# Moving the weighting of gathered pixels to ScalarE, parts of softplus to VectorE, and the order of the last image

## The chip, the cores and the metric

The kernel runs on one core of a Trainium2 chip. The core has five engines that run beside each other[...]: TensorE (PE, matrix products into PSUM), VectorE (DVE), ScalarE (ACT), GpSimd (POOL), and SyncE (SP, which here only issues transfers). Transfers are also issued from the queues of ACT and POOL. Each engine takes its instructions in the order in which the program lists them; one that waits holds up all behind it on the same engine. The metric is the time of one execution on the device in microseconds. The kernel before takes 9075.24 us, the median of nine runs between 9048.84 and 9094.0.

## The reference, cut to what matters

The input is four images of 96 channels and 64 x 64 pixels, so L = 4096 positions. Four layers are added to it in turn.

- Layer 0 normalises, projects to 192 channels, applies a 3 x 3 convolution and then a selective scan along four directions (rows, columns, and both reversed). With softplus written out, a step of it is

```
delta = softplus(dts + bias)          # max(p, 0) + log(1 + exp(-|p|))
h     = exp(delta * A) * h + (delta * u) * B      # 16 states per channel
y     = sum over the states of h * C
```

- Layer 1 is a deformable 3 x 3 convolution: for every pixel and each of nine taps an offset and a mask are computed, four neighbouring pixels are fetched and weighted, and the weighted sum goes through the weights of the tap:

```
samp = (1-wy)*(1-wx)*v00 + (1-wy)*wx*v01 + wy*(1-wx)*v10 + wy*wx*v11      # times the mask
out += einsum('bchw,oc->bohw', samp, weight[:, :, i, j])                   # for each of 9 taps
```

- Layer 2 is a Fourier transform along the positions with a pointwise network in it, then a feed-forward network whose operands are rounded to an 8-bit float. Layer 3 is a linear attention, then a second feed-forward network of the same kind.

## The kernel before, in words

**The scan sets the frame.** Layer 0's recurrence is cut into 1536 units: 4 images x 4 directions x 4 steps of 1024 positions x 24 groups of 8 channels x 16 states (128 partitions). For a unit, ACT fetches `da` (a transfer that repeats delta over the states) and takes its exponential (`decay`, L933), PE spreads delta times u into PSUM (`inflow`, L939), DVE multiplies by B in place (`enter`, L953) and runs the recurrence (`recur`, L961), POOL multiplies by C (`weigh`, L970, and the copy of the last state, L968), and PE sums over the states (`total`, L989). `hh`, the scan's output, has six buffers and `da` six; `db` in PSUM has two.

**Two streams lie beside it.** `ends()` runs `before` of layer 0 for images 0 to 3 (normalisation, convolution, projection, `steps`), and then layers 2 and 3 of image 0, 1, 2, 3 in turn. `middle()` runs, for each image, `behind` (the end of layer 0) and layer 1: `offsets`, `positions` and `sample`. An image can enter layers 2 and 3 only when layer 1 has sampled it.

**A planner writes the order.** The program's order on every engine is written when it is built. A `Clock` holds the planned end of each of PE, DVE, ACT and POOL; a step of a stream carries its planned cost (`cost(...)`), and is put in when the clock has room for it (`has_room`). A unit of the scan moves the clock on by at least `PACE`. The constant and the costs are not waits: they decide only which instructions stand between two units. What the streams have not done when the 1536 units are over stands after the scan, in the same manner (`alone`, `own_banks` is then set). `go()` offers the streams a step, `middle` first.

**`steps` (L752 to L815)** makes delta and delta times u for 512 positions of one direction (or of two half directions). PE gives the pre-activation `pd`; ACT takes |p|, exp, log(1 + e) into `lw`, 1 + e into `w1` and then `w1` - 1; POOL takes `w1` - e (the rounding of 1 + e, L780) and `lw` minus it (L781); DVE makes `rl` = max(p, 0) + `lw` (L783); POOL multiplies it by u into `ex` (L786 or L792); ACT and PE split that into three 16-bit parts. There are 192 such chains: 4 images x 8 pieces x 6. Nine of them start before the first unit of the scan.

**`sample` (L1284 to L1354)** handles an image in 96 chains, each of 128 pixels and three taps. POOL issues three indirect transfers (L1301), each of which brings 128 x 384 numbers (four neighbours x 96 channels) into `g`; one DVE multiplication over 128 x 1152 numbers applies the twelve weights per pixel (L1310); PE turns the result and adds the four neighbours (L1327), after the scan DVE adds them itself (L1314, L1315); ACT copies it to `st` (L1335). After six chains the nine taps are multiplied by the weights (L1343).

**The feed-forward networks (L1556 to L1600)** handle 512 positions at a time. POOL rounds the input to 8 bits (L1567) and the hidden values too (L1585).

Of the kernel before, what the change touches and what calls it, by code (L numbers as in the profile page):

```python
# [8 lines left out]
F32 = mybir.dt.float32  # L9
# [5 lines left out]
AF = mybir.ActivationFunctionType  # L15
ALU = mybir.AluOpType
# [184 lines left out]

MARGIN = 0.5

PACE = 4.7


class Clock:
# [138 lines left out]
class Net:  # L346
# [3 lines left out]
    def __init__(self, ctx, tc, ins):  # L350
        self.tc, self.nc, self.ins = tc, tc.nc, ins
        nc = self.nc
        self.const = ctx.enter_context(tc.tile_pool(name="const", bufs=1))
        self.dram = ctx.enter_context(tc.tile_pool(name="scratch", bufs=1, space=DRAM))
        self.psum = ctx.enter_context(tc.tile_pool(name="mm", bufs=3, space=PSUM))
        for name in ("vecs", "ident", "cen96", "grp3", "add4"):
            setattr(self, name, self.load(name, self.const))

        self.to_row = {}
        for n in (C, DI):  # L360
            t = self.to_row[n] = self.const.tile([128, 65], F32, name=f"to_row{n}")
            nc.vector.memset(t, 0.0)
            nc.vector.memset(t[:, 1:2], 1.0 / n)
        self.eps = self.const.tile([128, 1], F32, name="eps")
        nc.vector.memset(self.eps, 1e-5)
        self.one = self.const.tile([128, 1], F32, name="one")
        nc.vector.memset(self.one, 1.0)
        self.minus_one = self.const.tile([128, 1], F32, name="minus_one")
        nc.vector.memset(self.minus_one, -1.0)
        self.exp_and_log()  # L370

        self.sampled = set()
        self.clock, self.known, self.streams, self.stream = Clock(), {}, [], None

        self.own_banks = None
# [164 lines left out]
class Layer0:  # L540
# [211 lines left out]
    def steps(self, b, ks, j, us, dtw, sm, xdbl):  # L752

        net = self.net
        nc = net.nc
        cs = slice(j * CH, (j + 1) * CH)
        tk = f"{b}_{j}_" + "".join(str(k) for k in ks)
        both = len(ks) == 2

        def tile_of(name, bufs):  # L760
            return sm.tile([128, CH], F32, name=f"{name}{tk}", tag=name, bufs=bufs)

        yield wait(new=True, takes="ex lw")


        pd = net.mm(f"pd{tk}")
        for k in ks:
            q = k % 2
            o, m = (pd[64 * q : 64 * q + 64], slice(128, DI)) if both else (pd, slice(0, 128))
            nc.tensor.matmul(o, lhsT=dtw[:, k, m], rhs=xdbl[q, j], start=True, stop=True)  # L770
        ex = tile_of("ex", 3)
        nc.scalar.activation(ex, pd, AF.Abs)
        nc.scalar.activation(ex, ex, AF.Exp, scale=-1.0)
        lw, w1 = tile_of("lw", 1), tile_of("w1", 1)
        nc.scalar.activation(lw, ex, AF.Ln, bias=net.one)
        nc.scalar.activation(w1, ex, AF.Identity, bias=net.one)
        nc.scalar.activation(w1, w1, AF.Identity, bias=net.minus_one)  # L777
        yield cost(pe=2.2 if both else 1.1, act=3.4, holds=1, takes="rl")
        rl = tile_of("rl", 2)
        nc.gpsimd.tensor_sub(w1, w1, ex)  # L780
        nc.gpsimd.tensor_sub(lw, lw, w1)  # L781
        yield cost(pool=2.8, holds=1)
        nc.vector.scalar_tensor_tensor(rl, pd, 0.0, lw, ALU.max, ALU.add)  # L783
        yield cost(dve=0.7, frees="lw")
        if not both and ks[0] % 2:
            nc.gpsimd.tensor_mul(  # L786
                ex.rearrange("p (w h) -> p w h", h=H),
                rl.rearrange("p (w h) -> p w h", h=H),
                us[1][:, j * NR : (j + 1) * NR, :],
            )  # L790
        else:
            nc.gpsimd.tensor_mul(ex, rl, us[2 if both else 0][:, cs])  # L792
        parts = ((0, 64, ks[0], 128), (64, 128, ks[1], 128)) if both else ((0, 128, ks[0], 0),)
        for p0, p1, k, c0 in parts:
            nc.sync.dma_start(self.de_d[b][k][c0 : c0 + p1 - p0, cs], rl[p0:p1])
        yield cost(pool=1.4, takes="du", frees="rl")

        du = sm.tile([128, 3, CH], BF16, name=f"du{tk}", tag="du", bufs=2)
        nc.scalar.copy(du[:, 0, :], ex)
        yield cost(act=0.6, new=True)  # L800
        pr = net.mm(f"pr{tk}")
        nc.tensor.matmul(pr, lhsT=net.ident, rhs=ex, start=True, stop=False)  # L802
        nc.tensor.matmul(pr, lhsT=self.minus, rhs=du[:, 0, :], start=False, stop=True)
        nc.scalar.copy(du[:, 1, :], pr)
        yield cost(pe=1.5, act=0.6, holds=1, frees="ex")
        nc.tensor.matmul(
            pr, lhsT=self.minus, rhs=du[:, 1, :], start=False, stop=True, skip_group_check=True
        )
        nc.scalar.copy(du[:, 2, :], pr)
        yield cost(pe=0.4, act=0.6)  # L810
        for p0, p1, k, c0 in parts:
            dst = self.du_d[b][k][:, c0 : c0 + p1 - p0, cs]
            nc.sync.dma_start(dst.rearrange("s c t -> c s t"), du[p0:p1])
        self.ready.update((b, k, both, j) for k in ks)
        yield wait(frees="du")  # L815
# [300 lines left out]
class Layer1:  # L1116
# [23 lines left out]
    def image(self, b):  # L1140
        tc = self.net.tc
        with tc.tile_pool(name=f"l1i{b}", bufs=1, side="right") as ix:
            idx = ix.tile([128, 288], U32, name=f"idx{b}", tag="idx")
            wt = ix.tile([128, 288, 4], F32, name=f"wt{b}", tag="wt")
            yield from self.before(b, idx, wt)
            yield from self.sample(b, idx, wt)
        self.net.sampled.add(b)

# [135 lines left out]
    def sample(self, b, idx, wt):  # L1284
        net = self.net
        tc, nc = net.tc, net.nc
        with tc.tile_pool(name=f"l1g{b}", bufs=1, side="right") as gp:
# [4 lines left out]
            def taps(t, k0):  # L1292
# [6 lines left out]
                for k in range(3):  # L1299
# [5 lines left out]
                        in_offset=bass.IndirectOffsetOnAxis(ap=idx[:, n : n + 1], axis=0),  # L1305
                    )
                    yield cost(pool=1.5, wait=7.0 * (k == 2))
                g4 = g.rearrange("p k (c d) -> p (k c) d", d=C)
                w4 = wt[:, 9 * t + k0 : 9 * t + k0 + 3, :].rearrange("p k c -> p (k c)")
                nc.vector.tensor_mul(g4, g4, w4.unsqueeze(2).to_broadcast([128, 12, C]))  # L1310
                added = net.own_banks is not None
                if added:

                    nc.vector.tensor_add(g[:, :, : 2 * C], g[:, :, : 2 * C], g[:, :, 2 * C :])  # L1314
                    nc.vector.tensor_add(g[:, :, :C], g[:, :, :C], g[:, :, C : 2 * C])  # L1315
                first = q == 0 and k0 == 0
                yield cost(dve=2.7 if added else 1.8, new=True, takes="st" if first else "")
                if first:
                    sts[j] = gp.tile([C, 9, 256], F32, name=f"st{b}_{j}", tag="st")
                st = sts[j]  # L1320
# [210 lines left out]
class Ffn:  # L1531
# [23 lines left out]
    def run(self, b, t):  # L1555
        net, n = self.net, self.n  # L1556
        tc, nc = net.tc, net.nc
        with tc.tile_pool(name=f"fb{n}_{b}", bufs=1) as big, tc.tile_pool(name=f"fs{n}_{b}", bufs=2) as pool:
# [3 lines left out]
            def chunk(j):  # L1562
# [1 line left out]
                cs = slice(j * CH, (j + 1) * CH)  # L1564
                key = f"f{n}_{b}_{j}"
                xq = pool.tile([C, CH], F8, name=f"xq{key}", tag="xq")
                nc.gpsimd.tensor_copy(xq, tl[:, cs], saturate=False)  # L1567
                yield cost(pool=0.8, new=True, takes="h16")
                h16 = pool.tile([128, 3, CH], F16, name=f"h16{key}", tag="h16")
                for g in range(3):  # L1570
                    ph = net.mm(f"ph{key}_{g}")
# [10 lines left out]
                        nc.scalar.activation(h16[:, g], h16[:, g], AF.Relu, bias=self.bias[:, g : g + 1])  # L1582
                    yield cost(act=2.1, takes="h8")
                h8 = pool.tile([128, 3, CH], F8, name=f"h8{key}", tag="h8")
                nc.gpsimd.tensor_copy(h8, h16, saturate=False)  # L1585
                yield cost(pool=1.5, new=True, takes="o16", frees="h16")
                po = net.mm(f"po{key}")
                for g in range(3):
                    nc.tensor.matmul(po, lhsT=self.w2[:, g, :], rhs=h8[:, g], start=(g == 0), stop=(g == 2))
# [107 lines left out]
def layers23(net, x2, out):  # L1697
# [4 lines left out]
    with ExitStack() as ctx:  # L1702
# [21 lines left out]

        def go():

            return any([stream.step() for stream in reversed(streams)])

        def alone():

# [44 lines left out]
```

## Time and profile before

| | |
|---|---|
| median of nine runs | 9075.24 us |
| the profiled execution: its own time, and its span | 9094.23 us, 9092.4 us |
| busy: PE, DVE, ACT, POOL | 6614.3, 6969.0, 4183.0, 6363.9 us |
| first unit's recurrence starts, last one ends | 369 us, 7900 us |
| image 3: `offsets` starts, first gather, last operation of `sample` | 7955, 8071, 8539 us |
| transfer that loads image 3 for layers 2 and 3 starts | 8634 us |

The page of a profile gives for each group of instructions its line, engine and operation, the tiles it writes and reads, and then the busy time, the mean duration in ns, the idle time of the engine just before and what ended most of it. A table of stretches gives the busy time of each engine within a stretch of the span, then the granted TensorE clock, the share of the transfer engines and GB/s.

The trace shows three stages: up to 370 us layer 0 of the first image without the scan, up to 7900 us the scan with the streams beside it, and then some 1190 us of what is left.

### The profile page before, as it was taken

To read this page: it belongs to the slowest core of one execution; us is meant where nothing else is said; L and a number is where in the kernel's file an instruction comes from. 1 tells how busy PE (TensorE), PEld (TensorE's weight loads), DVE (VectorE), ACT (ScalarE), POOL (GpSimd) and SP (SyncE) were. 2 spreads that over 40 slices of the span, in tenths; PEclk is the share of its full clock that TensorE was granted. 3 is DMA by queue.
4 is the path that set the end of the run, shared out by engine and by line. 5 is a ranking of instruction groups with operands and counts; after the bars stand their busy time and mean duration, and the time that the engine had idled before them with its cause. 6 is when DMAs were issued, how large, how long until landed. Compare 5 with 4: busy or idle time off the path is not lost.

```text
span 9092.4 us, 93197 instructions
## 1 busy us (share of the span) xinstructions
PE 6614.3 (73%) x31960; PEld 2990.0 (33%) x31960; DVE 6969.0 (77%) x4932; ACT 4183.0 (46%) x5798; POOL 6363.9 (70%) x4755
## 2 busy tenths in 40 slices
PE   6664977697766668777667877777777677875687
PEld 2111311132222234211224554223454332463373
DVE  0367878887788889788789898988999999636514
ACT  4564667565554435556543334554333434321223
POOL 0486678766789989788799895765888967537501
PEclk8675977798778779877778888878888887876797
DMA  1466778777778788887778878677888776644210
GB/s 51 127 184 168 191 193 221 200 188 191 196 205 212 203 207 219 196 207 213 200 206 203 226 204 193 169 166 198 209 216 213 190 175 177 152 131 135 76 55 12
DMA packets 775967, 1608.21 MB, mean 177 GB/s; under 512 B 247809, under 2 KB 339357, under 8 KB 773382
## 3 DMA queue, kind: packets, MB, share of 16 engines
q10 hardware_dynamic: 244224, 843.17, 36.9%
q1 hardware_dynamic: 457542, 532.51, 21.8%
q0 software_dynamic: 73728, 226.57, 9.4%
q8 instruction: 255, 4.18, 0.2%
q14 instruction: 218, 1.79, 0.1%
HBM read 1345.62 MB, written 256.29 MB: 176 GB/s over the span
## 4 chain that ended last, share of the span: by engine, by line
PE 32%; DVE 20%; DMA 17%; POOL 12%; issue 10%; ACT 6%; SPq 2%; ACTq 1%; another core or an unknown queue 0%; DVEq 0%; POOLq 0%
DVE hh L961 9%; DVE db L953 6%; POOL hh L970 5%; PE pc L692 4%; PE ps L1327 3%; PE py L989 3%; PE f L1421 3%; PE db L939 3%; DMA du<-du 3%; DMA da<-de 3%; POOL g L1301 2%; PE pd L1343 2%; DVE g L1310 2%; DMA m<-in_dft 1%; PE pd L770 1%
## 5 line engine op out<-in xcount | busy, mean ns | idle before, releaser
L970 POOL TENSOR_TENSOR hh<-hh,bc 128x1024 f32<-128x1024 f32 x1536 | 3654.9, 2382 | 353.3 <-DVE hh L961 239.2
L961 DVE TENSOR_TENSOR_SCAN hh<-da,st,db 128x1024 f32<-128x1024 f32 x1152 | 2700.7, 2344 | 177.9 <-PE py L989 47.0
L953 DVE TENSOR_TENSOR db<-db,bc 128x1024 f32<-128x1024 f32 x1536 | 1864.5, 1214 | 511.7 <-PE db L939 497.8
L933 ACT ACTIVATE da<-da,w_al 128x1024 f32<-128x1024 f32 x1536 | 1739.7, 1147 | 843.4 <-DMA da<-de 383.1
L939 PE MATMUL db<-du,rep 96*128 96x512 bf16 x3072 | 1092.5, 445 | 791.8 <-DVE hh L961 711.9
L1301 POOL DMA_INDIRECT g<-table,idx x1152 | 1326.9, 1152 | 380.9 <-issue 227.0
L989 PE MATMUL py<-hh,w_fold 128*32 128x512 f32 x6144 | 1089.8, 741 | 85.1 <-POOL hh L970 57.7
L1327 PE MATMUL ps<-w_ident,g 128*96 128x128 f32 x3744 | 640.8, 334 | 504.1 <-issue 282.2
L961 DVE TENSOR_TENSOR_SCAN hh<-da,db 128x1024 f32<-128x1024 f32 x384 | 876.9, 2284 | 60.7 <-PE py L989 23.1
L939 PEld LDWEIGHTS <-rep 96*128 96x128 bf16 x3072 | 279.3, 106 | 1755.5 <-issue 1129.9
L1327 PEld LDWEIGHTS ps<-w_ident,g 128*96 128x96 f32 x3744 | 520.4, 155 | 780.2 <-issue 408.3
L1310 DVE TENSOR_TENSOR g<-g,wt 128x1152 f32<-128x1152 f32 x384 | 716.0, 1866 | 67.0 <-DMA g<-table,idx 62.6
L1335 ACT COPY st<-ps 96x384 f32<-96x384 f32 x384 | 181.8, 476 | 1271.4 <-PE ps L1327 1027.1
L968 POOL COPY st<-hh 128x1 f32<-128x1 f32 x1152 | 294.3, 255 | 509.6 <-DVE hh L961 464.9
L780 POOL TENSOR_TENSOR w<-w,ex 128x512 f32<-128x512 f32 x192 | 245.1, 1276 | 505.4 <-ACT w L777 504.7
L692 PE MATMUL pc<-pad,wc 96*128 96x512 f32 x1152 | 540.8, 609 | 48.3 <-DMA wc<-wc_d 44.0
L783 DVE SCALAR_TENSOR_TENSOR rl<-pd,lw 128x512 f32<-128x512 f32 x192 | 131.3, 684 | 425.7 <-POOL lw L781 411.1
L802 PE MATMUL pr<-ex,w_ident 128*128 128x512 f32 x384 | 290.8, 849 | 150.5 <-POOL ex L786 67.4
L1567 POOL CAST xqf<-fl 96x512 fp8e5<-96x512 f32 x64 | 46.9, 741 | 497.5 <-DVE fl L1525 458.8
L989 PEld LDWEIGHTS py<-hh,w_fold 128*32 128x32 f32 x6144 | 160.6, 120 | 606.4 <-issue 384.7
L770 PE MATMUL pd<-xd,w_dtw 103*64 103x512 f32 (+1 forms) x512 | 276.9, 817 | 65.8 <-DMA w_dtw<-in_dtw 33.1
L692 PEld LDWEIGHTS pc<-pad,wc 96*128 96x128 f32 x1152 | 215.8, 193 | 318.6 <-issue 295.9
(249 smaller groups left out, 9231.4 us busy)
## 6 DMA issues: line engine op xcount, KB each, us to landing
da<-de ACTq DMA_DIRECT2D x1536, 512.0 KB
du<-du SPq DMA_DIRECT2D x512, 192.0 KB
bc<-bcd SPq DMA_DIRECT2D x128, 512.0 KB
du<-du SPq DMA_DIRECT2D x128, 384.0 KB
y<-yb SPq DMA_DIRECT2D x384, 128.0 KB
de<-rl SPq DMA_DIRECT2D x128, 256.0 KB
m<-in_dft SPq DMA_DIRECT2D x128, 256.0 KB
ad<-y ACTq DMA_DIRECT2D x192, 128.0 KB
```

What stands on the lines that cost most here:

```text
L692: nc.tensor.matmul(pp, lhsT=wc[:, q, g * 128 : (g + 1) * 128], rhs=pad[:, r0 + dy : r0 + dy + NR, dx : dx + W], start=(q == 0), stop=(q == 8),
L770: nc.tensor.matmul(o, lhsT=dtw[:, k, m], rhs=xdbl[q, j], start=True, stop=True)
L933: self.net.nc.scalar.activation(u.da, u.da, AF.Exp, scale=self.al[:, a : a + 1])
L939: self.net.nc.tensor.matmul(db[:, h, :], lhsT=self.rep[:96, u.s % 4, :], rhs=u.du[u.s // 4][:, h * CH : (h + 1) * CH], start=True, stop=True,)
L953: self.net.nc.vector.tensor_mul(u.db, u.db, u.bc[:, 0, :])
L961: nc.vector.tensor_tensor_scan(u.along(u.hh), u.along(u.da), u.along(u.db), first, ALU.mult, ALU.add)
L968: self.net.nc.gpsimd.tensor_copy(u.state[:, u.n : u.n + 1], u.hh[:, last : last + 1])
L970: self.net.nc.gpsimd.tensor_mul(u.hh, u.hh, u.bc[:, 1, :])
L989: nc.tensor.matmul(py[p0 : p0 + 32], lhsT=self.fold[:, u.i, :], rhs=hc[:, h * CH : (h + 1) * CH], start=u.sums["add"] is None and u.i == 0 ...
L1301: nc.gpsimd.indirect_dma_start(out=g[:, k, :], out_offset=None, in_=self.tables[b % 2], in_offset=bass.IndirectOffsetOnAxis(ap=idx[:, n : ...
L1310: nc.vector.tensor_mul(g4, g4, w4.unsqueeze(2).to_broadcast([128, 12, C]))
L1327: nc.tensor.matmul(pt[:, k, :], lhsT=g[:, k, c * C : (c + 1) * C], rhs=net.ident, is_transpose=True, start=(c == 0), stop=(c == corners - 1),)
```

## The change

There are five parts.

1. In `sample`, the one DVE multiplication of 128 x 1152 becomes twelve ACT instructions of 128 x 96, each with the weight of its pixel as a per-partition scale. The weights are the same.
2. In `steps`, the ACT instruction that takes 1 from `w1` goes; the subtraction of 1 and of e becomes one DVE instruction (L778 of the new file) in the place of POOL's. POOL keeps the subtraction from `lw`. The product of delta and u (L785, L791) goes from POOL to DVE.
3. After the scan, the two roundings to 8 bits in the feed-forward networks are done by DVE in the place of POOL. Beside the scan POOL keeps them.
4. Once sampling of the last image begins, `go()` offers `ends` (layers 2 and 3) a step first, and `middle` after it.
5. `PACE` goes from 4.7 to 4.5, and the planned costs follow the parts above.

In the two built programs ACT has 4416 instructions more (4608 added, 192 removed), POOL 448 fewer and DVE 63 more. All four images' gathers, 864 beside the scan and 288 after it, stand on the same side of the scan's end in both. Layers 2 and 3 of image 2 begin behind unit 1468 before the change, and behind the last unit, 1536, after it; of image 1 only the very last addition of layer 3 still comes after the scan.

```diff
-PACE = 4.7
+PACE = 4.5
...
         nc.scalar.activation(w1, ex, AF.Identity, bias=net.one)
-        nc.scalar.activation(w1, w1, AF.Identity, bias=net.minus_one)
-        yield cost(pe=2.2 if both else 1.1, act=3.4, holds=1, takes="rl")
+        yield cost(pe=2.2 if both else 1.1, act=2.7, holds=1, takes="rl")
         rl = tile_of("rl", 2)
-        nc.gpsimd.tensor_sub(w1, w1, ex)
+        nc.vector.scalar_tensor_tensor(w1, w1, -1.0, ex, ALU.add, ALU.subtract)
+        yield cost(dve=0.7, holds=1)
         nc.gpsimd.tensor_sub(lw, lw, w1)
-        yield cost(pool=2.8, holds=1)
+        yield cost(pool=1.3, holds=1)
         nc.vector.scalar_tensor_tensor(rl, pd, 0.0, lw, ALU.max, ALU.add)
         yield cost(dve=0.7, frees="lw")
         if not both and ks[0] % 2:
-            nc.gpsimd.tensor_mul(
+            nc.vector.tensor_mul(
...
         else:
-            nc.gpsimd.tensor_mul(ex, rl, us[2 if both else 0][:, cs])
+            nc.vector.tensor_mul(ex, rl, us[2 if both else 0][:, cs])
...
-        yield cost(pool=1.4, takes="du", frees="rl")
+        yield cost(dve=0.7, takes="du", frees="rl")
...
             yield from self.before(b, idx, wt)
+            self.net.sampling_last = b == B - 1
             yield from self.sample(b, idx, wt)
...
-                g4 = g.rearrange("p k (c d) -> p (k c) d", d=C)
-                w4 = wt[:, 9 * t + k0 : 9 * t + k0 + 3, :].rearrange("p k c -> p (k c)")
-                nc.vector.tensor_mul(g4, g4, w4.unsqueeze(2).to_broadcast([128, 12, C]))
+                for k in range(3):
+                    for c in range(4):
+                        pixel = g[:, k, c * C : (c + 1) * C]
+                        n = 9 * t + k0 + k
+                        nc.scalar.activation(pixel, pixel, AF.Identity, scale=wt[:, n, c : c + 1])
+                    if k < 2:
+                        yield cost(act=0.7)
                 added = net.own_banks is not None
...
-                yield cost(dve=2.7 if added else 1.8, new=True, takes="st" if first else "")
+                yield cost(dve=1.0 * added, act=0.7, new=True, takes="st" if first else "")
...
-                nc.gpsimd.tensor_copy(xq, tl[:, cs], saturate=False)
-                yield cost(pool=0.8, new=True, takes="h16")
+                if net.own_banks:
+                    nc.vector.tensor_copy(xq, tl[:, cs], saturate=False)
+                    yield cost(dve=0.4, new=True, takes="h16")
+                else:
+                    nc.gpsimd.tensor_copy(xq, tl[:, cs], saturate=False)
+                    yield cost(pool=0.8, new=True, takes="h16")
...
-                nc.gpsimd.tensor_copy(h8, h16, saturate=False)
-                yield cost(pool=1.5, new=True, takes="o16", frees="h16")
+                if net.own_banks:
+                    nc.vector.tensor_copy(h8, h16, saturate=False)
+                    yield cost(dve=1.0, new=True, takes="o16", frees="h16")
+                else:
+                    nc.gpsimd.tensor_copy(h8, h16, saturate=False)
+                    yield cost(pool=1.5, new=True, takes="o16", frees="h16")
...
-            return any([stream.step() for stream in reversed(streams)])
+            return any([stream.step() for stream in (streams if net.sampling_last else streams[::-1])])
```

## The prediction

> **What bounds the kernel now.** I read the busy times first, then the stages, then what DVE waits for inside the scan, and then the rows of the instructions that change. The page's first part:
>
> ```profile
> PE 6614.3 (73%) x31960; PEld 2990.0 (33%) x31960; DVE 6969.0 (77%) x4932; ACT 4183.0 (46%) x5798; POOL 6363.9 (70%) x4755
> ```
>
> No engine is full over the span, so the stages decide. The next view cuts the span where the scan begins (370), where it ends (7900), where image 3's gathers begin (8071) and end (8539). Columns: length, then busy time and count of PE, weight loads, DVE, ACT, POOL, then clock, share of the transfer engines, GB/s.
>
> ```profile
> 0.00:370.00 370.00, 221.49 (x452) 84.85 (x453) 26.39 (x53) 163.88 (x203) 39.10 (x38) 0.79 0.22 65
> 370.00:7900.00 7530.00, 5528.65 (x25808) 2319.00 (x25807) 6430.84 (x4194) 3704.59 (x4965) 5893.77 (x4342) 0.81 0.77 198
> 7900.00:8071.00 171.00, 146.63 (x1276) 105.48 (x1276) 41.87 (x68) 48.95 (x91) 19.07 (x22) 0.86 0.39 97
> 8071.00:8539.00 468.00, 270.04 (x1162) 178.52 (x1159) 299.07 (x374) 91.61 (x185) 351.53 (x305) 0.65 0.46 133
> 8539.00:9093.00 554.00, 447.54 (x3269) 302.15 (x3268) 170.84 (x245) 173.99 (x355) 60.40 (x50) 0.85 0.11 32
> ```
>
> In the scan DVE is busy 6431 of 7530 us (85%); POOL 78%, PE 73%, ACT 49%. A unit takes 7530/1536 = 4.90 us, and DVE's two instructions of a unit 2.33 + 1.21 of it:
>
> ```profile
> L961 DVE TENSOR_TENSOR_SCAN hh<-da,st,db 128x1024 f32<-128x1024 f32 x1152 | 2700.7, 2344 | 177.9 <-PE py L989 47.0
> L953 DVE TENSOR_TENSOR db<-db,bc 128x1024 f32<-128x1024 f32 x1536 | 1864.5, 1214 | 511.7 <-PE db L939 497.8
> ```
>
> So the pace is that of DVE's queue: 4.19 us of work and 0.72 us of idle time per unit. The waits of DVE (total, times, longest) say what the idle time is:
>
> ```profile
> DVE db L953 <- PE db L939: 497.8, 226, 20.9
> DVE rl L783 <- POOL lw L781: 411.1, 76, 216.3
> ...
> DVE g L1310 <- DMA g<-table,idx: 62.6, 32, 6.9
> ```
>
> The second is 260 before the scan and, by the gaps ahead of L783 after 370 us, 151 inside it. After the scan no engine is full: until 8539 image 3's gathers are made (POOL 75% busy) with image 2 beside them, and then image 3 goes alone through layers 2 and 3, a chain in which PE's share is largest.
>
> **Part 1, the weighting.** Two stretches of the one line, in and after the scan:
>
> ```profile
> 370.00:7900.00 7530.00, 585.87 (x288) 0.81 0.77 198
> 7900.00:9093.00 1193.00, 130.14 (x96) 0.78 0.28 81
> ```
>
> The scan loses 586 us of DVE work (2.03 us each), the end 130 (1.36 each). The new ACT instruction is in no row. Two ACT rows with one per-partition operand give it: 722 ns for 512 numbers (L777) and 1147 for 1024 (L933), so 0.83 ns a number, and 722 - 416 x 0.83 = 377 ns for 96. In ACT's timeline L776 begins 0.62 us after L775, which takes 0.72, so independent neighbours overlap by 0.09: 0.28 each, 3.4 us a chain. Ends: 0.25 (the row of `om`, 250 ns for 108 numbers) and 0.38; I take 0.28. That is 288 x 3.4 = 980 us on ACT in the scan and 325 after it. In the scan ACT would be busy 3705 + 980 less 135 (the removed instruction, 183 x 0.74) = 4550 of some 7370 us, 62%: the cover is ACT's idle time. Without cover each chain would hold up the exponentials `da` and the transfers that ACT issues; the third rival prices that.
>
> **Part 2, `steps`.** POOL loses two instructions of three, 1.28 and about 1.4 us; in the scan 183 x 2.7 = 490 us. DVE gains two, both with two inputs in SBUF. Ends: 0.68 us (L783, one input in PSUM) and about 2.0 (0.68 and more than half of a POOL multiplication of 2.38). A row of the same kind is near, 96x512 with two SBUF inputs in the scan:
>
> ```profile
> 370.00:7900.00 7530.00, 42.52 (x32) 0.81 0.77 198
> ```
>
> That is L1598, 1.33 us each; L783 has 0.68 and L1310 2.03 in the scan against 1.36 after it, so both pay some 0.65 us for POOL's company. The Trainium skill (SBUF — State Buffer, Who interferes with whom) states the rule that speaks against this part: a DVE instruction with two SBUF inputs and a GpSimd instruction that reads SBUF exclude each other for the whole instruction. With POOL busy 73% of the time then, in pieces of 2.38 us, a random arrival waits 0.73 x 1.19 = 0.87 (an estimate): 1.55 us each. By the rule the scan gains 366 x 1.55 = 567 us of DVE work, by the row 366 x 1.3 = 476. I take the row: it is this kernel's own company.
>
> **DVE's sum in the scan.** -586 + 476 - 20 (the first half of image 2's layer 2, moved behind the scan) = -130; by the rule -39; uncontended, -357. The idle time: with half of POOL's work gone from the chain ahead of L783 some of its 151 us go, but the new instruction at L778 waits at the head of DVE's queue for ACT, with the next unit's L953 and L961 behind it. I take -30, between -150 and +115 (in stretches where DVE has less to do per unit, as 1024 to 1310 us, it idles 0.85 us a unit, against 0.45 where it is full). The scan: 7530 - 160 = 7370, its end at 7740 (the 370 us before stay: nine chains there lose POOL time and gain DVE time, where both are idle).
>
> **Part 5, `PACE`.** It moves work only: image 2's first half of layer 2, and so all of its layers 2 and 3, stand behind the scan.
>
> **Parts 3 and 4 and the end.** The stage before the first gather keeps its 171 us (`middle` is still offered first there). The stage with the gathers had POOL as fullest, 351 of 468 us. Now ACT has 325 + 46 (copies to `st`) + 90 (image 2) = 460 us; POOL's 331; and image 2 brings a longer piece of its chain. At the share POOL had (75%) the stage would take 615, at 90% 510; with the copies independent of each other I take 550, so 82 more. The last stage: 24 pairs of roundings, 0.74 + 1.55 on POOL (L1567, L1585), become about 0.46 + 1.0 on DVE (the CAST of 128x576, L1262, 460 ns; 16-bit L1578, 515 ns for a third of the size, at most), but four pieces run beside each other, so I take 15 of the 20 us off: 539. The end: 171 + 550 + 539 = 1260, against 1193.
>
> **The sum.** 370 + 7370 + 1260 = 9000 against a span of 9092: -92. The profiled execution itself, 9094.23, lies 19 above the median 9075.24; applied to the median, 9075 - 92 = 8983. I predict 8983 us, 1.0% less.
>
> **The rivals.**
> First: *the gain is larger*, since POOL's lighter load takes the contention and the waits with it. For: POOL loses 490 us in the scan and nothing else is at 85%. DVE -357, idle -100, the end +40: 9075 - 417 = 8660 at most; half of it, 8865, is what I give this case.
> Second: *the gain is given back at the end*. PE needs about 390 us (its groups' sum, overlaps counted twice) for the moved half of layer 2 and is the fullest engine of the last stages. If the stage with gathers takes 615 and the scan only loses what was moved: 9075 - 130 + 132 = 9077, no change.
> Third, and slower: *ACT becomes the scan's bound where gathers are made*. Place: the sampling stretches (some 900 of the 1536 units), where ACT would carry 3.0 to 4.0 us per unit in an order in which it also waits for each gather, for `hh` before a `da` buffer is refetched, and issues that transfer (0.52 us each on its queue). For: L933 already waits:
>
> ```profile
> ACT da L933 <- DMA da<-de: 383.1, 162, 9.7
> ```
>
> Against: exponentials stand two units ahead, some 9 us, and transfers five. Price: a chain that delays the recurrence by 1 us costs 288 us; from 0.32 us per chain on it eats the 92 us. I give 1 us with half of it hidden by DVE's own idle time: 8983 + 190 = 9170. A gain by the removed POOL work can't outweigh that, since POOL isn't what the recurrence waits for (5.9 us in all).
>
> **How the numbers follow.** My forecast 0.50, larger gain 0.14, no change 0.10, slower 0.26. The likeliest one's own range is 8890 to 9080 (the rule's price for part 2, +91; idle time -120; the last stages +-60). The other cases reach from 8780 to 9250; leaving one in ten at either end gives 8820 to 9180. About 0.2% is what a measurement of this kernel can tell from no change. Faster: 0.47 of the forecast, 0.14 of the larger gain and 0.01 of the third = 0.62. Same: 0.03 and 0.05 = 0.08. Slower: 0.25 and 0.05 = 0.30.
>
> **What would show it.** Right: the last recurrence ends near 7740; DVE's busy time in the scan is near 6300, L778 and the products at 1.2 to 1.4 us; the ACT instruction has 0.37 us and ACT in the scan some 4550; the gathers' stage is the longer one, near 550. Wrong: L961 waits for `da` by more than 100 us in all (third rival); the two DVE rows below 0.9 us (first); a stage with gathers beyond 600 us (second); or PE, which waits for the weighted `g` in its own order, being late with `db`, so that L953's wait for it grows by more than the 92 us.

## The result and the profile after

The changed kernel takes 8981.15 us, the median of ten runs between 8946.04 and 8998.96; the ratio to the kernel before is 0.9891, with a 95% interval from 0.9876 to 0.9906. The forecast was 8983. The total is right to 2 us; its parts are not, and the experiments are about the parts.

The profiled execution has a span of 8980.5 us. First the page's busy times of the kernel after, then its stages with the columns used before: to the first recurrence (355), to the last (7645), to image 3's first gather (7834), to the end of its `sample` (8457), to the end.

```profile
PE 6651.5 (74%) x31960; PEld 2937.8 (33%) x31960; DVE 6692.2 (75%) x4995; ACT 5240.5 (58%) x10214; POOL 5561.9 (62%) x4307
```

```profile
0.00:355.00 355.00, 215.49 (x452) 84.48 (x453) 40.58 (x71) 155.59 (x193) 14.84 (x19) 0.81 0.23 68
355.00:7645.00 7290.00, 5459.76 (x24592) 2178.83 (x24591) 6251.42 (x4239) 4440.55 (x8179) 5229.71 (x3975) 0.81 0.77 203
7645.00:7834.00 189.00, 149.09 (x1192) 97.17 (x1190) 42.67 (x74) 55.64 (x103) 22.55 (x22) 0.84 0.40 100
7834.00:8457.00 623.00, 416.91 (x2588) 306.22 (x2585) 188.62 (x320) 424.52 (x1416) 287.14 (x289) 0.70 0.37 111
8457.00:8981.00 524.00, 410.29 (x3144) 271.05 (x3144) 168.87 (x294) 164.19 (x323) 7.66 (x2) 0.87 0.11 34
```

| stage | before | after | forecast |
|---|---|---|---|
| up to the first recurrence | 369 | 355 | 370 |
| scan | 7531 | 7290 | 7370 |
| last recurrence to first gather | 171 | 189 | 171 |
| gathers of image 3 | 468 | 623 | 550 |
| what remains | 553 | 524 | 539 |

The scan lost 241 us, 81 more than forecast, and the end gained 144, 76 more than forecast. In the scan DVE's busy time fell by 179 us (6431 to 6251), POOL's by 664 (5894 to 5230; 130 of these because the gathers, L1301, went from 1000 to 870 us, which the forecast did not have), and ACT's rose by 736 (3705 to 4441). The two instructions of a unit and the new ACT instruction, from the page's groups of the kernel after:

```profile
L960 DVE TENSOR_TENSOR_SCAN hh<-da,st,db 128x1024 f32<-128x1024 f32 x1152 | 2701.4, 2345 | 231.7 <-PE py L988 80.5
L952 DVE TENSOR_TENSOR db<-db,bc 128x1024 f32<-128x1024 f32 x1536 | 1864.0, 1214 | 532.5 <-PE db L938 522.1
...
L1312 ACT ACTIVATE g<-g,wt 128x96 f32<-128x96 f32 x4608 | 1282.8, 365 | 170.3 <-DVE hh L960 55.8
```

A weighting instruction has 365 ns, against 377 worked out; the group's busy time over its count is 0.28 us, as taken. DVE's waits now (total, times, longest):

```profile
DVE db L952 <- PE db L938: 522.1, 219, 21.0
DVE g L1318 <- ACT g L1312: 365.5, 83, 42.0
DVE w L778 <- ACT w L775: 279.9, 53, 212.5
```

The wait on GpSimd's `lw`, 411 us before, is down to 26; VectorE waits for ScalarE's part of the softplus instead, with 72 us of idle time in the scan ahead of the `steps` instructions where there were 151. The second line lies behind the scan: VectorE waits there for the pixels that ScalarE weights.

The moved softplus instructions are dearer than alone and cheaper than forecast. Three stretches of the kernel after, one for each of L778, L785 and L791 (only the scan):

```profile
355.00:7645.00 7290.00, 148.15 (x182) 0.81 0.77 203
...
355.00:7645.00 7290.00, 115.75 (x60) 0.81 0.77 203
...
355.00:7645.00 7290.00, 134.42 (x123) 0.81 0.77 203
```

That is 0.81, 1.93 and 1.09 us, 398 us in all or 1.09 each, where the row of L1598 had led to 1.3, and the rule of the Trainium skill (SBUF — State Buffer, Who interferes with whom), with GpSimd met at random, to an estimate of 1.55. Ahead of the scan the same two products took 1.03 (L785, which reads u column by column) and 0.69 (L791). The rule agrees with the trace; the random meeting does not. Least, median and longest time of two instructions of a chain, the first with both inputs in SBUF, the second with one in PSUM:

```profile
L778 DVE SCALAR_TENSOR_TENSOR w<-w,ex x192: 665/683/2827, 277.7 to 4716.2; 128x512 f32<-128x512 f32 x192
L782 DVE SCALAR_TENSOR_TENSOR rl<-pd,lw x192: 659/680/695, 279.8 to 4738.6; 128x512 f32<-128x512 f32 x192
```

In the scan, 147 of the 182 instructions of L778 overlap no arithmetic of GpSimd and take 0.68 us; the 35 that do take 1.36 on average. L782 takes 0.68 either way (37 and 146 of them). GpSimd is busy in 72% of the scan, with arithmetic in 57%, but its arithmetic is under way at the start of L778 in 16% of the cases only: the place of an instruction in the order decides what company it has. The products meet more of it: 76 of 123 of L791 (1.34 us against 0.69 alone) and 46 of 60 of L785 (2.20 against 1.05).

### The profile page after: what moved, and what is told of

It is laid out like the page before. It is cut to its first block, busy times and chain, and to the rows that moved or that the text cites. A ratio compares the mean times of both kernels' runs of the same rounds, so it can differ in the third digit from the quotient of the medians.

```text
span 8980.5 us, 97776 instructions
## 1 busy us (share of the span) xinstructions
PE 6651.5 (74%) x31960; PEld 2937.8 (33%) x31960; DVE 6692.2 (75%) x4995; ACT 5240.5 (58%) x10214; POOL 5561.9 (62%) x4307
## 4 chain that ended last, share of the span: by engine, by line
PE 34%; DVE 27%; DMA 16%; ACT 10%; issue 7%; POOL 3%; SPq 2%; ACTq 1%; DVEq 0%; another core or an unknown queue 0%; POOLq 0%
DVE hh L960 14%; DVE db L952 8%; DMA du<-du 5%; PE pc L691 4%; ACT g L1312 4%; PE py L988 4%; PE ps L1331 3%; PE db L938 3%; PE f L1425 3%; DMA da<-de 2%; PE pd L1347 2%; POOL hh L969 1%; ACT da L932 1%; DMA bc<-bcd 1%; PE h L1466 1%
## 5 line engine op out<-in xcount | busy, mean ns | idle before, releaser
L960 DVE TENSOR_TENSOR_SCAN hh<-da,st,db 128x1024 f32<-128x1024 f32 x1152 | 2701.4, 2345 | 231.7 <-PE py L988 80.5
L952 DVE TENSOR_TENSOR db<-db,bc 128x1024 f32<-128x1024 f32 x1536 | 1864.0, 1214 | 532.5 <-PE db L938 522.1
L932 ACT ACTIVATE da<-da,w_al 128x1024 f32<-128x1024 f32 x1536 | 1741.3, 1146 | 617.7 <-DMA da<-de 275.9
L1301 POOL DMA_INDIRECT g<-table,idx x1152 | 1153.2, 1001 | 548.9 <-issue 186.4
L1312 ACT ACTIVATE g<-g,wt 128x96 f32<-128x96 f32 x4608 | 1282.8, 365 | 170.3 <-DVE hh L960 55.8
L988 PE MATMUL py<-hh,w_fold 128*32 128x512 f32 x6144 | 1057.2, 762 | 26.8 <-POOL hh L969 9.0
L960 DVE TENSOR_TENSOR_SCAN hh<-da,db 128x1024 f32<-128x1024 f32 x384 | 877.2, 2284 | 70.1 <-PE py L988 25.2
L1331 PE MATMUL ps<-w_ident,g 128*96 128x128 f32 x3744 | 682.7, 325 | 315.4 <-ACT g L1312 166.2
L780 POOL TENSOR_TENSOR lw<-lw,w 128x512 f32<-128x512 f32 x192 | 244.2, 1272 | 815.9 <-DVE w L778 797.7
L1331 PEld LDWEIGHTS ps<-w_ident,g 128*96 128x96 f32 x3744 | 487.2, 142 | 671.5 <-ACT g L1312 294.0
L967 POOL COPY st<-hh 128x1 f32<-128x1 f32 x1152 | 232.4, 202 | 709.1 <-DVE hh L960 660.1
L1318 DVE TENSOR_TENSOR g<-g 128x576 f32<-128x576 f32 x96 | 72.9, 759 | 393.7 <-ACT g L1312 365.5
L778 DVE SCALAR_TENSOR_TENSOR w<-w,ex 128x512 f32<-128x512 f32 x192 | 155.1, 808 | 280.7 <-ACT w L775 279.9
L1347 PE MATMUL pd<-st,wdc 96*128 96x256 f32 x1152 | 317.5, 426 | 7.1 <-ACT st L1339 3.4
```

The source lines that it names most:

```text
L932: self.net.nc.scalar.activation(u.da, u.da, AF.Exp, scale=self.al[:, a : a + 1])
L952: self.net.nc.vector.tensor_mul(u.db, u.db, u.bc[:, 0, :])
L960: nc.vector.tensor_tensor_scan(u.along(u.hh), u.along(u.da), u.along(u.db), first, ALU.mult, ALU.add)
L988: nc.tensor.matmul(py[p0 : p0 + 32], lhsT=self.fold[:, u.i, :], rhs=hc[:, h * CH : (h + 1) * CH], start=u.sums["add"] is None and u.i == 0 ...
L1301: nc.gpsimd.indirect_dma_start(out=g[:, k, :], out_offset=None, in_=self.tables[b % 2], in_offset=bass.IndirectOffsetOnAxis(ap=idx[:, n : ...
L1312: nc.scalar.activation(pixel, pixel, AF.Identity, scale=wt[:, n, c : c + 1])
```

## The experiments

The theory at the start: VectorE's queue sets the scan's pace, so that what is taken from it shortens the scan; ScalarE's queue sets the end where gathers are made. The rivals: the relief of GpSimd is what pays; the order written with another `PACE` is what pays; at the end the order of the two streams, or TensorE, is what counts. Every stage below is in us (to within 1), from the profiled execution of the run; a ratio is to the kernel before, timed beside the run. Its medians in the four groups of runs were 9075, 9089, 9101 and 9098 us, and a profiled execution lies up to 28 us from the median of its kernel, so a difference of some 30 us between stages of two runs means little.

| kernel | ratio, 95% interval | to first unit | scan | end |
|---|---|---|---|---|
| before | 1 | 369 | 7531 | 1193 |
| after | 0.9891 (0.9876 to 0.9906) | 355 | 7290 | 1335 |
| weights_only | 1.0126 (1.0095 to 1.0157) | 370 | 7463 | 1376 |
| steps_only | 1.0077 (1.0046 to 1.0109) | 357 | 7643 | 1134 |
| weights_back | 0.9999 (0.9973 to 1.0025) | 357 | 7608 | 1110 |
| steps_back | 1.0134 (1.0086 to 1.0182) | 368 | 7267 | 1590 |
| plan_only | 1.0055 (1.0026 to 1.0084) | 371 | 7429 | 1362 |
| split_enter | 1.0131 (1.0086 to 1.0175) | 357 | 7517 | 1348 |
| pace_back | 0.9918 (0.9886 to 0.9951) | 356 | 7418 | 1216 |
| order_back | 1.0074 (1.0046 to 1.0102) | 357 | 7296 | 1504 |
| casts_back | 0.9889 (0.9843 to 0.9935) | 356 | 7300 | 1344 |
| dve_at_end | 0.9759 (0.9726 to 0.9793) | 356 | 7276 | 1201 |
| end_pace | 0.9792 (0.9752 to 0.9833) | 354 | 7452 | 1086 |
| true_cost | 0.9815 (0.9765 to 0.9865) | 358 | 7288 | 1284 |

**The weighting alone.** Part 1 put into the kernel before:

```diff
-                nc.vector.tensor_mul(g4, g4, w4.unsqueeze(2).to_broadcast([128, 12, C]))
+                for k in range(3):
+                    for c in range(4):
+                        pixel = g[:, k, c * C : (c + 1) * C]
+                        n = 9 * t + k0 + k
+                        nc.scalar.activation(pixel, pixel, AF.Identity, scale=wt[:, n, c : c + 1])
+                    if k < 2:
+                        yield cost(act=0.7)
...
-                yield cost(dve=2.7 if added else 1.8, new=True, takes="st" if first else "")
+                yield cost(dve=1.0 * added, act=0.7, new=True, takes="st" if first else "")
```

> The kernel before with the weighting of the gathered pixels moved to ScalarE, and nothing else. If VectorE's queue alone sets the scan's pace, 586 us of its work go there and nothing comes in its place: the scan, 7530 us before, shortens by 400 to 480, the end grows by some 60 to 80 since ScalarE is then the fullest engine there; in all 8650 to 8750 us. If instead the relief of GpSimd by the changed softplus steps is what shortens the scan, or its order written with the smaller PACE, then this kernel stays at 9030 to 9080.

It is slower than before: 9205.25 us, ratio 1.0126. Neither the theory's 8650 to 8750 nor the rival's 9030 to 9080 held. The scan's stretch of this kernel:

```profile
370.00:7834.00 7464.00, 5610.01 (x26280) 2324.53 (x26279) 5932.07 (x3933) 4599.92 (x8430) 5658.40 (x4342) 0.81 0.79 200
```

VectorE lost 499 us of work in the scan and the scan 67 us. Its wait for the spread over the whole run:

```profile
DVE db L953 <- PE db L939: 743.6, 325, 25.4
```

VectorE now waits 744 us for the spread `db`, where it was 498, and the idle time ahead of all its instructions in the scan went from 1099 to 1531 us. TensorE makes `db` in its own order, and the prediction named the reason that it might be late: it stands and waits for the weighted `g`, which it turns. The waits ahead of that turning within the scan, before and then here, say otherwise:

```profile
PE ps L1327 <- issue: 151.0, 75, 7.3
PE ps L1327 <- DVE g L1310: 139.4, 56, 15.7
```

```profile
PE ps L1331 <- ACT g L1312: 171.2, 74, 10.9
```

With all smaller waits TensorE stands 220 us there, less than the 355 before. In the 740 us in which VectorE sits idle ahead of the multiplication by B, the trace has TensorE at work for 580 (400 of 490 before; the ends of its matrix products are modelled): with `db` itself, and with work of the streams. So what left VectorE's queue as work came back as waiting, mostly for an engine that was itself at work. The end is 183 us longer: its stage with the gathers has 612 us.

**The softplus part undone.** Part 2 taken out of the changed kernel, costs and all:

```diff
+        nc.scalar.activation(w1, w1, AF.Identity, bias=net.minus_one)
...
-        nc.vector.scalar_tensor_tensor(w1, w1, -1.0, ex, ALU.add, ALU.subtract)
-        yield cost(dve=0.7, holds=1)
+        nc.gpsimd.tensor_sub(w1, w1, ex)
         nc.gpsimd.tensor_sub(lw, lw, w1)
-        yield cost(pool=1.3, holds=1)
+        yield cost(pool=2.8, holds=1)
...
-            nc.vector.tensor_mul(ex, rl, us[2 if both else 0][:, cs])
+            nc.gpsimd.tensor_mul(ex, rl, us[2 if both else 0][:, cs])
```

> The changed kernel with the softplus steps as before: GpSimd does two more instructions per chain and VectorE two fewer. If VectorE's queue sets the pace, 398 us leave it in the scan (155 + 120 + 138 us in the changed profile, the parts before the scan left out) and the scan shortens by 200 to 330: 8700 to 8800 us. If GpSimd's load counts as much, with its 490 us back on an engine that is then busy 78% of the scan, the time is 9000 to 9100.

9215.14 us, above both ranges, on the rival's side. VectorE has 406 us less to do in the scan (5845 against 6251) and the scan takes the same time, 7267 us. But less stands in it: with GpSimd's long steps the planner puts less of the streams beside the units (image 0 is loaded for layers 2 and 3 at unit 1021, in the changed kernel at 915), and the first gather of image 3 comes 375 us after the scan, not 189. The end has 1590 us. So this run mixes two things, the load and the order.

**The same order, the old engines.** To separate them, the planned costs and with them the order of the changed kernel were kept, and only the engines of the softplus work put back:

```diff
+        nc.scalar.activation(w1, w1, AF.Identity, bias=net.minus_one)
...
-        nc.vector.scalar_tensor_tensor(w1, w1, -1.0, ex, ALU.add, ALU.subtract)
+        nc.gpsimd.tensor_sub(w1, w1, ex)
         yield cost(dve=0.7, holds=1)
...
-            nc.vector.tensor_mul(ex, rl, us[2 if both else 0][:, cs])
+            nc.gpsimd.tensor_mul(ex, rl, us[2 if both else 0][:, cs])
```

> The changed kernel with its planned costs, so with exactly its order of instructions, but the softplus work on the engines of the kernel before: ScalarE takes 1 again, GpSimd subtracts and multiplies. If it is the written order that pays (a chain that is planned shorter lets the streams get further beside the scan), the time stays within 80 us of the changed kernel's: 8950 to 9060. If the load of GpSimd itself is what counts, VectorE waits for it in its own order and the scan is 200 us longer or more: 9150 to 9300.

9160.26 us, within the second theory's range, though the scan is 138 us longer and not 200: the engines count, not the order alone. The scan's stretch, and VectorE's waits over the run:

```profile
371.00:7800.00 7429.00, 5517.42 (x24565) 2186.42 (x24591) 5894.60 (x3876) 4570.31 (x8361) 5642.67 (x4340) 0.80 0.79 199
```

```profile
DVE db L955 <- PE db L941: 687.5, 285, 26.8
DVE rl L785 <- POOL lw L783: 539.5, 97, 216.0
```

Against the changed kernel VectorE has 357 us less work in the scan, and its idle time there is 1534 us where it is 1039, 495 more: 200 ahead of the `steps` instructions, 163 ahead of the multiplication by B, 90 ahead of the recurrence. The 200 are the wait for GpSimd's `lw` in the place of ScalarE's `w`. How the other two come about is not shown: TensorE stands 225 us ahead of GpSimd's product (`pr` for `ex`), but it stood 159 ahead of VectorE's. VectorE's recurrence and its multiplication by B have the same mean times in both runs (2345 and 1214 ns), so the heavier load of GpSimd reaches them as waiting and not as slower instructions. The work that the change gave to VectorE costs less than the waiting did: at the same order part 2 is worth 138 us of scan, 16 ahead of it and 27 at the end.

**The softplus part alone**, put into the kernel before:

> The kernel before with the softplus part alone: VectorE gains some 400 us of work in the scan, GpSimd loses 490. If VectorE's queue sets the pace, the scan grows by 300 us or more: 9300 to 9450. If the pace is that of the written order, and the planner, rid of GpSimd's long steps, puts more of the streams beside the scan, the scan stays within 150 us of 7530 and the end gets shorter by 100 to 200 us: 8900 to 9050.

9162.11 us, between the two theories. The edit is part 2 of the change as shown in the diff. VectorE gained 357 us of work in the scan; its idle time fell from 1099 to 855, and the scan grew by 112 us. The end lost 58. Some of both is work that moved: TensorE has 110 us more in this scan. Alone, the part loses.

**VectorE's load per unit, by itself.** In the changed kernel the multiplication by B is cut in two halves:

```diff
-        self.net.nc.vector.tensor_mul(u.db, u.db, u.bc[:, 0, :])
+        for h in range(2):
+            hs = slice(h * CH, (h + 1) * CH)
+            self.net.nc.vector.tensor_mul(u.db[:, hs], u.db[:, hs], u.bc[:, 0, hs])
```

> The changed kernel with VectorE's multiplication by B cut into two halves, each of 128x512: planned costs as before, some 0.13 us more of VectorE's time per unit by the rows (0.67 twice against 1.21), 200 us over the scan. If VectorE's queue sets the pace, the scan grows by 150 to 250 us: 9130 to 9230. If the pace is set by what the units wait for and VectorE's idle 0.68 us per unit hides it, by less than 80: 8980 to 9060.

9221.56 us, in the range of VectorE's queue as the pace. The scan's stretch:

```profile
357.00:7874.00 7517.00, 5516.19 (x24592) 2203.10 (x24591) 6577.24 (x5776) 4450.01 (x8179) 5205.08 (x3975) 0.80 0.76 197
```

326 us more on VectorE make the scan 227 us longer; the idle time takes up 99. So work that is added does lengthen the scan, by seven tenths of it here. The two halves are 254 us of it; 83 are the products of `steps`, which take 1.82 us each here and 1.37 in the changed kernel: GpSimd's arithmetic is under way at the start of 112 of the 183, where it was 72. It is not spread evenly: the units 0 to 63 went from 4.95 to 5.83 us each and the units 192 to 255 from 4.61 to 5.31, together 101 of the 227 us, and both are stretches where softplus chains run and VectorE has little idle time (27 and 21 us of some 300): there 50 and 48 us of work made 57 and 45 of time. In a sampling stretch (units 832 to 1023) 30 us of work came in and the pace changed from 4.42 to 4.41.

**`PACE` undone.**

```diff
-PACE = 4.5
+PACE = 4.7
```

> The changed kernel with PACE 4.7 in the planner. If the constant only moves work between the scan and the end, the scan grows by some 30 to 60 us and the end, which loses half of image 2's layer 2, shrinks by about as much: 8960 to 9010 us. If the smaller constant made the scan denser, the scan is over 100 us longer and the time 9050 to 9150.

9006.17 us; the intervals of the two ratios overlap, so no difference is shown. The scan is 128 us longer, more than the 30 to 60 expected, and the end 119 us shorter: the constant moves work between them. What it moves holds 26 us of VectorE's work and 137 of TensorE's, and the forecast had moved 20 us, VectorE's part alone; beside the scan it took 128.

**Sampling first at the end.** Part 4 undone:

```diff
-            return any([stream.step() for stream in (streams if net.sampling_last else streams[::-1])])
+            return any([stream.step() for stream in streams[::-1]])
```

> The changed kernel with sampling offered first to the end, as before. If layers 2 and 3 of image 2 are what the end waits for, they finish later and the time grows by 30 to 100 us: 9010 to 9080. If sampling is what it waits for, the gathers' stage falls below 600 us and the time to 8900 to 8970.

9159.26 us, more than either theory gave it. The end's three stages in this run:

```profile
7652.00:7842.00 190.00, 149.05 (x1200) 97.33 (x1200) 42.77 (x74) 55.54 (x103) 22.55 (x22) 0.82 0.40 99
7842.00:8469.00 627.00, 303.08 (x2014) 238.70 (x2012) 140.41 (x234) 376.11 (x1301) 277.47 (x288) 0.63 0.37 107
8469.00:9157.00 688.00, 538.52 (x3714) 343.81 (x3710) 221.68 (x379) 218.15 (x438) 11.52 (x3) 0.85 0.10 29
```

The stage with the gathers takes 627 us with sampling first and 623 with sampling second. Offered first, layers 2 and 3 of image 2 fit in for nothing (TensorE is busy 417 us in it, not 303), and what remains takes 524 us and not 688. Both runs have `PACE` 4.5; with 4.7, where the first half of that layer 2 is done beside the scan, the order alone was not run.

**The weighting on VectorE after the scan.** The changed kernel with part 1 beside the scan only:

```diff
+                if net.own_banks is not None:
+                    g4 = g.rearrange("p k (c d) -> p (k c) d", d=C)
+                    w4 = wt[:, 9 * t + k0 : 9 * t + k0 + 3, :].rearrange("p k c -> p (k c)")
+                    nc.vector.tensor_mul(g4, g4, w4.unsqueeze(2).to_broadcast([128, 12, C]))
+                else:
...
-                yield cost(dve=1.0 * added, act=0.7, new=True, takes="st" if first else "")
+                yield cost(dve=2.7 * added, act=0.7 * (not added), new=True, takes="st" if first else "")
```

> The changed kernel, but with the weighting on VectorE again after the scan, where VectorE is busy 189 of 623 us while image 3 is sampled and ScalarE 425. If ScalarE's queue is what makes that stage 623 us long, it falls to 480 to 540 and the time to 8840 to 8900; the scan stays as it is. If TensorE or the chain of image 2 sets the stage, or the order of the two streams, it stays near 600 and the time at 8950 to 8980.

8863.11 us, in the range of ScalarE's queue. Its last two stages, with the gathers and after them:

```profile
7822.00:8331.00 509.00, 400.98 (x2653) 288.67 (x2652) 329.68 (x442) 137.83 (x290) 341.11 (x289) 0.81 0.46 135
8331.00:8834.00 503.00, 392.48 (x3068) 268.94 (x3066) 153.23 (x268) 151.40 (x298) 7.66 (x2) 0.84 0.12 35
```

ScalarE's busy time in the stage falls from 425 to 138 us and the stage from 623 to 509; the scan is as it was. In the chain that ended last through this stage ScalarE's weighting had 29.1% in the changed kernel; here VectorE's has 2.8%. ScalarE, with 68% of the stage, was what made it long. This version beats both kernels: 0.9759 of the kernel before.

**The same with `PACE` 4.7.**

> The kernel with the weighting on VectorE after the scan, with PACE 4.7. If the constant only moves work, the scan is some 125 us longer and the end as much shorter: 8830 to 8890, no difference from PACE 4.5. If the end gains more now that ScalarE is free in it, 8780 to 8830.

8911.53 us, above both ranges, where the kernel before, timed beside it, took 9101; the interval of the ratio, 0.9752 to 0.9833, overlaps the one of 4.5, so again no difference is shown. The scan is 176 us longer and the end 115 shorter.

**The planner told the right cost.** In the version with the weighting on VectorE at the end, `act=0.7` becomes 1.1, 1.1 and 1.2 for the three parts of a chain:

> The kernel with the weighting on VectorE after the scan, with the planner told what ScalarE's twelve instructions take (3.4 us a chain where it was told 2.1). If TensorE stands waiting for late weighted pixels and so brings its spreads late, VectorE's wait for them falls from 522 us by 80 or more and the time to 8780 to 8850. If that lateness is hidden, the planner only places less beside the scan: 8860 to 8930.

8934.28 us, just above the second range; the interval of its ratio overlaps that of dve_at_end. VectorE's idle time ahead of the multiplication by B fell by 53 us in the scan (504 to 451), and all of its idle time did not fall (1031 to 1065); the scan is the same and the end 82 us longer, with less placed beside the scan. Pricing ScalarE right in the planner brought no gain, and nine tenths of the wait for `db` stayed.

**The weighting on VectorE throughout**, with parts 2 to 5 as changed:

> The changed kernel with the weighting on VectorE throughout, so with parts 2 to 5 alone. If moving the weights pays beside the scan (VectorE rid of 586 us there), the scan is 150 to 350 us longer; the end is 120 to 250 shorter, since VectorE weights there and more of layers 2 and 3 stands beside the scan: 8950 to 9100. If the move paid nothing anywhere, the scan is within 60 us of 7290 and the time near 8750 to 8850.

9091.33 us, ratio 0.9999, in the range of a move that pays. The scan is 318 us longer than the changed kernel's, and the end 225 shorter. Part of both is work that moved: image 2 is loaded for layers 2 and 3 at unit 1436 here, and behind the scan in the changed kernel. The run with `PACE` 4.7 (pace_back) is the closer partner, with unit 1453 and nearly the same work of TensorE in the scan (5597 us against 5653). Against it the scan is 190 us longer for 483 us of VectorE's work. So the move of the weights does pay beside the scan where part 2 is in; alone it had paid 67 for 499.

**The roundings on GpSimd.** Part 3 undone:

> The changed kernel with the two roundings on GpSimd in the end too. If they lie on the chain of the last image, 8990 to 9030; if four pieces beside each other hide them, within 15 us of the changed kernel.

9004.7 us. That is in the first range, but the kernel before, timed beside it, took 9098: the ratio is 0.9889 against 0.9891, and its interval holds the changed kernel's. Its gathers' stage has 635 us and the rest 520: the part is worth nothing that shows.

## Why the prediction was right, and where it was not

**The total** is right by luck: it is the sum of errors that cancel. The scan lost 81 us more than forecast and the start 14, the end gained 76 more, which leaves the span 20 us shorter than forecast. That the median is right to 2 us is a second chance: the forecast took 19 us off, since the profiled execution before lay so far above its median; the changed kernel's, 8982, lies at its own.

**"The pace is that of DVE's queue"** held in one direction. VectorE is the engine that lengthens the scan when it is given more (split_enter), but the forecast took 130 us of work off the queue and left its idle time nearly alone (-30). The measured change is -179 of work and -60 of idle time, and the -60 is a difference of large terms. Part 1 alone turned 499 us of work into 432 of waiting (weights_only). Part 2, at the same order, turned 495 of waiting into 357 of work (plan_only). The idle time depends on how long the other engines keep the head of VectorE's queue waiting; it isn't a constant per unit.

**Part 1's ScalarE price** was right (0.28 us each), and in the scan ScalarE was the cover it was said to be: L960 waited for `da` 26 us in the scan, so the third rival's mechanism does not show. (That rival's price had a slip: half of 1 us for each of 288 chains is 144 us, not 190.) That TensorE might come late with `db` had been named as a sign of being wrong; in the whole change that wait grew by 24 us only, in part 1 alone by 246.

**Part 2** was booked as a loss of 476 us of VectorE's time, with some idle time off. The instructions measured 398. The row of L1598 and the rule were both about the right thing, GpSimd's company, but not about how often it is met: L1598 met it in 25 of its 32 cases in the scan, the rule was worked out for an engine busy 73% of the time, and L778 met it in 35 of 182. The part's worth lies in the other term, the waiting for GpSimd's chain. The first rival named GpSimd's relief; contention on VectorE's units was no part of it (their times did not change), waiting was.

**Part 4** had no term of its own. The forecast of 539 us for what remains holds only if layers 2 and 3 of image 2 find room in the stage with the gathers. They did (524); with sampling first they do not (688, order_back), and the end is 169 us longer, 1.8% of the time by the ratios. So the largest single term at the end was a condition that the forecast never priced.

**The stage with the gathers** was put too short, 550 us against 623, which is past the second rival's mark of 600. ScalarE's work in it was forecast as 460 us and measured 425; what failed is the share, 68% where 75 to 90% had been assumed. The mechanism of that rival, TensorE as the fullest engine, was not the cause: the stage follows ScalarE (dve_at_end). Nor was its size right: the 390 us of TensorE's work are a sum in which overlapping products count several times; TensorE's busy time behind the scan rose by 112 us (864 to 976).

**Part 3** was booked with 15 us; the runs show none. **Part 5** moves work, as said; that the moved half of layer 2 takes 128 us of scan for 26 us of VectorE's work was missed, and it comes back at the end.

**Where the gain lies.** Four runs have nearly the same work beside the scan (TensorE 5529 to 5638 us of it; image 2 loaded for its layers at units 1427 to 1467), and they differ in parts 1 and 2:

| scan | weights on VectorE | weights on ScalarE |
|---|---|---|
| softplus as before | 7531 (before) | 7463 (weights_only) |
| softplus as changed | 7643 (steps_only) | 7418 (pace_back) |

The weights take 68 us off alone and 225 beside the softplus part; that part adds 112 alone and takes 45 off beside the weights, each to within some 30 us. Together they are worth 113 us; the two single effects add up to a loss. At the end pace_back is 23 us above the kernel before. No difference is shown between the two values of `PACE`. Of the single parts, the weights alone lose 1.3% and the softplus steps alone 0.8%; all but part 4 lose 0.7% (order_back, with `PACE` 4.5), and with image 2 offered first at the end they gain 1.1%.

What stays open: why VectorE's waits for `db` grew by so much with the weights alone. The trace shows TensorE mostly at work in that time and not standing ahead of the turned pixels, which points to its queue as the next limit; but none of the runs changed TensorE's load or the place of `db` in its order by itself.

## What to carry to other kernels

In a queue that runs in order, busy time and waiting at its head are one budget, but they don't move alike: give a full engine more work and the time grows; take work off it and the time shrinks only if what it next waits for is early enough. Before a part is priced as work moved to a full engine, look at what that engine waits for on the engine it is moved from: here doing it was cheaper than waiting for it. A cover is a matter of stage: ScalarE had room for the weights beside the scan and none behind it, so an assignment made per stage (0.976) beat the one for all (0.989). At the end the stream that still had the most to do was best offered first.

## What the runs showed of the hardware

- VectorE instructions with both inputs in SBUF get longer when they overlap arithmetic of GpSimd: 0.68 us alone and 1.36 with it (L778, 147 and 35 cases in the scan). With one input in PSUM (L782) they take 0.68 either way.
- Two equal products on VectorE with both inputs in SBUF differ by their access, also without that company: reading u column by column (L785) took 1.05 us in the scan and 1.03 ahead of it, reading it in order (L791) 0.69 in both.
- GpSimd's indirect transfers (L1301) get longer beside VectorE's multiplications over `g`, which have two inputs in SBUF. Before, 1152 ns each; with the weights alone moved to ScalarE, 986:

```profile
L1301 POOL DMA_INDIRECT g<-table,idx x1152 | 1326.9, 1152 | 380.9 <-issue 227.0 <-ACT d L1430 71.4 <-PE ps L1327 15.3
```

```profile
L1301 POOL DMA_INDIRECT g<-table,idx x1152 | 1136.2, 986 | 544.0 <-ACT st L1339 193.5 <-issue 175.7 <-ACT fl L478 76.4
```

GpSimd's own load is not the cause of this: with the softplus part alone, which lightens it, they take 1149 ns, and with the changed order and the softplus work back on GpSimd (plan_only) 992. In dve_at_end they take 1.00 us in the scan and 1.17 behind it, where VectorE weights again.
- Twelve ScalarE instructions of 96 numbers in a row take 3.30 us in the timeline, against 1.36 for the one VectorE instruction after the scan. By the rows of 365 ns for 96 numbers and 1146 for 1024 (L932) a number costs 0.84 ns, so the 1152 numbers are some 1.0 us of the 3.30 (an estimate); the rest is paid per instruction.
